# Distances of a graph layer: the right factor by one transpose and masked copies, and one weight load placed a product later

## The chip, the cores and the metric

The kernel runs on one core of one Trainium2 chip. The metric is the device time of one execution in microseconds (us). Before the change three runs gave 1744.81, 1745.28 and 1748.23 us, median 1745.28 us.

A core has five engines that work side by side, each with its own queue of instructions in order: TensorE (PE; its weight loads are shown as PEld), VectorE (DVE), ScalarE (ACT), GpSimd (POOL) and SyncE (SP, which here only issues DMAs). [...]

## The reference, cut to what matters

The layer takes x (32 graphs, 512 nodes, 256 features) and a 0/1 adjacency matrix per graph. After a layer norm and a ReLU (h), three things are made of h and fed to a GRU-like gate block:

```
s     = h @ w_se.T + b_se                       # 3 numbers per node
sq    = sum(s*s, -1)
dist  = sq[:, :, None] + sq[:, None, :] - 2 * einsum('bnd,bmd->bnm', s, s)
A     = exp(-dist) * adj                        # 512 x 512 per graph
x_nmp = A @ relu(h @ w_msg.T + b_msg)
x_conv = relu(bn2(conv17(relu(bn1(conv1(h))))) + h)
gi = [x_conv, x_nmp] @ w_ih.T + b_ih ;  gh = h @ w_hh.T + b_hh
r, z = sigmoid(gi_r + gh_r), sigmoid(gi_z + gh_z)
out = x + (1-z) * tanh(gi_n + r*gh_n) + z*h
```

All arithmetic is float32. The change concerns how -dist is formed for one graph, and where one load of w_hh stands.

## The kernel before, in words

**Stages.** The 32 graphs are worked in two groups of 16. For each group `first_part` makes h, its transpose hT (tile `hT`, PE transposes `phT`), the first convolution (`conv1`, L434) and a transform along the nodes (`windows_to_freq`, L449). Then `nodes` runs over the group's graphs: messages (`message`, L551), distances, the aggregation with A (`aggregate7`, a product of seven block products with sums on POOL, L655), and, spread between, the 40 `product`s of the transformed convolution (L498), which need weights `wt` loaded from DRAM by SP (L460). Group 0 leaves four products over; they run inside group 1's `first_part`. A last stage computes the gates for 16 pairs of graphs.

**Order.** In these stages the order of instructions on every engine is the order of the program text (a manual schedule). The tool puts in the waits. So an instruction that waits holds all that stand behind it on its engine.

**The distances of one graph.** The 512 nodes are held as 4 chunks of 128; node features lie with nodes on partitions. `message` computes for each chunk the 256 message features and the 3 numbers s in one product (L551), and DVE adds the biases into `st` (L553) and into the message tile (L554); ACT applies ReLU to two chunks at a time (L555). `features` squares s on DVE (L562) and lets ACT lay out two tiles: `fl` (L563), 32 columns per chunk of which 9 are used (s, s squared, and a constant -0.5), and `fr` (L565, two copies), the same kind of rows for the right side, written four times over, once for each place the left chunk can have: 4 x 128 columns. `factors` turns `fl` by one PE transpose (L570), evicted by ACT to `sl` (L572), and `fr` by **four** PE transposes (L575), one per chunk, evicted by one ACT copy to `sr`, 128x512 (L577). Row group 32*mc of `sl` then holds the 9 rows of left chunk mc, and the same rows of `sr` hold the right side of all 512 nodes. `exponents` runs four matmuls `pd` over 9 rows each (L593); they start at partitions 0, 32, 64 and 96. ACT takes the exponential (L599), DVE multiplies with the transposed adjacency (L582, L603).

**Around the start of `nodes`** the text order is: all of message of the first graph; its `features`; half of the message of the second graph; `factors` of the first; `by_chunks` of the third (two ACT copies, L536); the other half of the second's message; `features` of the second; `exponents` of the first; and then the loop, which starts with `factors` of the second. In the loop `factors` of a graph stands before one or two products and a message, and its `exponents` behind them.

**Around the load.** In group 1's `first_part` a list `left` holds the four products left over, cut into five fills. With b0 the group's first graph, the text order is:

```
fill 1: load_unit(u2), prepare(u1)
load_x(b0+2)  [SP];  transpose_h(b0);  statistics(b0+1)
fill 2: combine.pop(0), product(u0), prepare(u2)
normalise(b0+1);  statistics(b0+2)
fill 3: product(u1), load_unit(u3)
load_x(b0+3)  [POOL's DMA queue];  conv1(b0)
fill 4: prepare(u3), product(u2)
normalise(b0+2);  transpose_h(b0+1)
fill 5: product(u3)
statistics(b0+3);  transpose_h(b0+2);  normalise(b0+3);  conv1(b0+1);  windows_to_freq(b0)
```

`prepare` does two sums on POOL (L465 `wsum`, needs `wt`; L478 `both`), which the last third of `product` needs. `statistics` ends with a power on POOL (L393). The first entry of `combine` issues one thing: the load of w_hh in four DMAs of 192 KB on POOL's queue (L211), for weight sums that POOL makes later.

Of the kernel before, what the change touches and what calls it, by code (L numbers as in the profile page):

```python
# [11 lines left out]
FP = mybir.dt.float32  # L12
AF = mybir.ActivationFunctionType
ALU = mybir.AluOpType

P = 128
# [146 lines left out]
def gnn_layer(  # L163
# [15 lines left out]
    nc = tc.nc  # L179
    B, N, D = x.shape  # L180
    KT = w2T.shape[1]
    PAD = KT // 2
    NS = w_seT.shape[1]
    DC = D // P
    NC = N // P
# [7 lines left out]
    consts = ctx.enter_context(tc.tile_pool(name="consts", bufs=1))  # L193
    dram = ctx.enter_context(tc.tile_pool(name="dram", bufs=1, space=bass.MemoryType.DRAM))
    psum = ctx.enter_context(tc.tile_pool(name="psum", bufs=8, space=bass.MemoryType.PSUM))
    pools = {}
    outer = ExitStack()
    work = pools["work"] = outer.enter_context(tc.tile_pool(name="work", bufs=2, reuse_waits="tile"))
    early = outer.enter_context(tc.tile_pool(name="early", bufs=1, reuse_waits="tile"))
    wts = outer.enter_context(tc.tile_pool(name="wts", bufs=3, reuse_waits="tile"))  # L200

    def bank(name):
        return psum.tile([P, N], FP, tag="bank", name=name)

    X, ADJ, XN, HT, HQ, H1, MSG, A, NMP, ST, SL, SR = ({} for _ in range(12))
# [12 lines left out]
    ident = consts.tile([P, P], FP, name="ident")  # L218
# [14 lines left out]
    at, cols, n = {}, {}, 0  # L233
# [15 lines left out]

    def vectors():  # L250

        for h in range(2):
            rows = slice(64 * h, 64 * (h + 1))
            nc.gpsimd.tensor_copy(vech[rows].rearrange("p (m e) -> p e m", e=DC),
                                  vec2[rows].rearrange("p e (m h) -> p e m h", h=2)[..., h])
        for name in VEC:
            at[name] = vech[:, cols[name]]
        nc.gpsimd.tensor_add(brz, at["b_ih"][:, : 2 * DC], at["b_hh"][:, : 2 * DC])
        batch_norm("bn2", scale2, shift2, nc.gpsimd)

    def batch_norm(k, scale, shift, engine):
        engine.tensor_scalar(scale, at[k + "_v"], BN_EPS, None, op0=ALU.add)
        nc.gpsimd.tensor_tensor(scale, scale, minus_half[:, :DC], op=ALU.pow)
        engine.tensor_mul(scale, scale, at[k + "_g"])
        engine.tensor_mul(shift, at[k + "_m"], scale)
        engine.tensor_sub(shift, at[k + "_b"], shift)
# [9 lines left out]
    row1 = [bank(f"row1_{i}") for i in range(2)]  # L276
    shift1_row = early.tile([P, D], FP, name="shift1_row")
    def bn1_row(i, v, ones, diags):
        for c in range(DC):
            diag = diags[:, i, c, :]  # L280
            nc.scalar.activation(diag, ident, AF.Copy, scale=v[:, c : c + 1])
            nc.tensor.matmul(row1[i][:, c * P : (c + 1) * P], ones, diag, start=True, stop=True)
# [17 lines left out]
    bmsg = early.tile([P, D + NS], FP, name="bmsg")  # L300
# [16 lines left out]

    fl = early.tile([P, NC, 32], FP, name="fl")  # L320
    fr = early.tile([P, NC, 4, 32], FP, name="fr")
    nc.vector.memset(fl, 0.0)
    nc.vector.memset(fr, 0.0)
    nc.vector.memset(fl[:, :, 2 * NS : 3 * NS], -0.5)
    nc.vector.memset(fr[:, :, :, NS : 2 * NS], -0.5)


    WD = dram.tile([ROWS, D * D + 4 * D], FP, name="wd")
# [197 lines left out]
    def by_chunk(t):  # L526

        return t.rearrange("p (g c k) -> p c g k", g=4, c=NC)

    def chunks(t):  # L530
        return t.rearrange("p (c g k) -> p c g k", g=4, c=NC)

    def by_chunks(b):
# [2 lines left out]
            nc.scalar.copy(chunks(HQ[b][:, ic, :]), by_chunk(HT[b][:, ic, :]))  # L536
        del HT[b]

    def message(b, halves=range(2)):
        if 0 in halves:  # L540
            ST[b] = pools["nodes"].tile([P, 2, NC, NS], FP, tag="st", name=f"st_{b}", bufs=2)
            MSG[b] = pools["nodes"].tile([P, NC, D], FP, tag="msg", name=f"msg_{b}", bufs=3)
        hq = HQ[b]
        h = NC // 2
        for c0 in (h * k for k in halves):
            m = MSG[b][:, c0 : c0 + h, :]
            for j in range(h):
                c = c0 + j
                p = bank(f"pm_{b}_{c}")
                for ic in range(DC):  # L550
                    nc.tensor.matmul(p[:, : D + NS], hq[:, ic, c * P : (c + 1) * P], wmsg[:, ic, :],  # L551
                                     start=(ic == 0), stop=(ic == DC - 1))
                nc.vector.tensor_add(ST[b][:, 0, c, :], p[:, D : D + NS], bmsg[:, D:])  # L553
                nc.vector.tensor_add(m[:, j, :], p[:, :D], bmsg[:, :D])  # L554
            nc.scalar.activation(m, m, AF.Relu)  # L555
        if 1 in halves:
            del HQ[b]

    def features(b):

        st = ST.pop(b)
        nc.vector.tensor_mul(st[:, 1], st[:, 0], st[:, 0])  # L562
        nc.scalar.copy(fl[:, :, : 2 * NS].rearrange("p c (k n) -> p k c n", n=NS), st)  # L563
        for k, at in enumerate((0, 2 * NS)):
            nc.scalar.copy(fr[:, :, :, at : at + NS], st[:, k, :, None, :].to_broadcast([P, NC, 4, NS]))  # L565

    def factors(b):

        p = bank(f"psl_{b}")
        nc.tensor.transpose(p[:, :P], fl.rearrange("p c k -> p (c k)"), ident)  # L570
        t = SL[b] = pools["nodes"].tile([P, P], FP, tag="sl", name=f"sl_{b}", bufs=2)
        nc.scalar.copy(t, p[:, :P])  # L572
        p = bank(f"psr_{b}")
        for c in range(NC):
            nc.tensor.transpose(p[:, c * P : (c + 1) * P], fr[:, c].rearrange("p g k -> p (g k)"), ident)  # L575
        t = SR[b] = pools["nodes"].tile([P, N], FP, tag="sr", name=f"sr_{b}", bufs=2)
        nc.scalar.copy(by_chunk(t), chunks(p))  # L577

    def turn(b, mcs):
        for mc in mcs:  # L580
# [5 lines left out]
    def exponents(b):  # L586

        A[b] = pools["nodes"].tile([P, NC, N], FP, tag="A", name=f"A_{b}", bufs=2)
        sl, sr = SL.pop(b), SR.pop(b)
        pd = [bank(f"pd_{b}_{mc}") for mc in range(NC)]  # L590
        for mc in range(NC):
            rows = slice(32 * mc, 32 * mc + 3 * NS)
            nc.tensor.matmul(pd[mc], sl[rows, :], sr[rows, :], start=True, stop=True)  # L593
        for mc in range(NC):
            if b in in_banks:
                EXP[b, mc] = pd[mc]
            else:
                EXP[b, mc] = A[b][:, mc, :]
            nc.scalar.activation(EXP[b, mc], pd[mc], AF.Exp)  # L599
# [552 lines left out]
    def first_part(g, freq, between, left=()):  # L1152
# [6 lines left out]
        if g == 0:  # L1159
            t = XN[b0] = pools["first"].tile([P, NC, D], FP, tag="xn", name="rows", bufs=2)  # L1160
            ones, diags = t[:, 0, :P], t[:, 1:3, :].rearrange("p i (c m) -> p i c m", m=P)
            nc.vector.memset(ones, 1.0)

            for _ in range(5):
                nc.tensor.matmul(row1[1][:, : 2 * P], ident, fr.rearrange("p c g k -> p (c g k)")[:, : 2 * P], start=True, stop=True)
            batch_norm("bn1", scale1, shift1, nc.gpsimd)
            bn1_row(0, scale1, ones, diags)
            bn1_row(1, shift1, ones, diags)
# [24 lines left out]
        for b in range(b0, b1):  # L1193
            if b + 3 < b1:
                load_x(b + 3, nc.sync if b < 3 else nc.gpsimd)
            if b == b0:
# [13 lines left out]
                xf, last_two = freq(g), two  # L1210
# [62 lines left out]
    with tc.tile_pool(name="freq", bufs=1) as fpool:  # L1273
# [3 lines left out]
        with phase("first", "gen"):  # L1277
# [23 lines left out]
            with tc.manual_schedule():  # L1301
                xf = first_part(0, freq_tile, between)
# [4 lines left out]
        def nodes(g, xf, units, last, following=()):  # L1307
# [45 lines left out]
            for i, b in enumerate(todo):  # L1353
# [24 lines left out]
                if more:  # L1378
                    factors(more[0])
# [32 lines left out]
        with phase("pw", "ahead"):  # L1412
            with phase("seven", "nodes"):
                with tc.manual_schedule():
                    nodes(0, xf, range(UNITS - LEFT), GB, range(UNITS - LEFT, UNITS - LEFT + 2))
            with phase("first", "sums"):
                combine = combine_weights()

                def between(b):

                    if b == GB - 3:
                        for u in range(3):
                            load_unit(1, u)
                    two = [partial(sum_unit, pools["pw"], 1, b - GB + 3)] if b > GB - 3 else []
                    return combine[b - 2] if 1 < b <= len(combine) + 1 else [], two


                pw, (u0, u1, u2, u3) = pools["pw"], range(UNITS - LEFT, UNITS)
                left = [[partial(load_unit, 0, u2, pools["sums"]), partial(prepare, pw, 0, u1, xf)],
                        [*combine.pop(0), partial(product, pw, 0, u0, xf), partial(prepare, pw, 0, u2, xf)],  # L1430
                        [partial(product, pw, 0, u1, xf), partial(load_unit, 0, u3)],
                        [partial(prepare, pw, 0, u3, xf), partial(product, pw, 0, u2, xf)],
                        [partial(product, pw, 0, u3, xf)]]
                prepare(pw, 0, u0, xf)
                with tc.manual_schedule():
                    xf = first_part(1, freq_tile, between, left)
            with phase("seven", "nodes"):
                with tc.manual_schedule():
                    nodes(1, xf, range(UNITS), GB - 3)
# [92 lines left out]
```

## Time and profile before

| | us |
|---|---|
| median of three runs | 1745.28 |
| the profiled execution | 1746.26 |
| its span, first to last instruction | 1744.5 |
| PE busy | 1727.1 |
| DVE busy | 1311.0 |
| POOL busy | 1083.0 |
| ACT busy | 672.6 |

In time order of that span: group 0's `first_part` up to about 157 us, its `nodes` to about 430, group 1's `first_part` to about 549, its `nodes` to about 831, then the gates. The profile page lists busy times, a chain of waits that leads back from the last instruction, and groups of instructions by line; a timeline lists instructions in order with, in brackets, the idle time before them and what ended it. A matmul's busy time includes its way through the array; what a matmul costs on a full PE is the distance from its start to the next one's start.

### The profile page before, as it was taken

The numbers are of one execution on the slowest core, as the hardware profiler recorded it, in microseconds if no ns is written. First come the engines' busy times: TensorE is split into PE (matmuls) and PEld (weight loads), VectorE is DVE, ScalarE is ACT, GpSimd is POOL, SyncE is SP. The second block draws the span as 40 slices with busy tenths as digits, with TensorE's granted clock in tenths as the row PEclk, the third lists the DMA queues.
The fourth block names the chain that finished last, engine by engine and source line by source line (L and its number), as shares of the span: only waits on it lengthen the run. The fifth ranks groups of instructions, "written<-read, shape, count | busy, mean of one in ns | idle before, by whom it ended". The sixth has DMA issues, their size and how long they took to land.

```text
span 1744.5 us, 24392 instructions
## 1 busy us (share of the span) xinstructions
PE 1727.1 (99%) x8006; PEld 1332.3 (76%) x8006; DVE 1311.0 (75%) x2598; ACT 672.6 (39%) x1543; POOL 1083.0 (62%) x1071
## 2 busy tenths in 40 slices
PE   9999999999999999999999999999999999999998
PEld 6677888888898888886877787778777787778754
DVE  7885787777896667766477788777877788777867
ACT  4556545543445544544323231323223232323221
POOL 3431787777655677767866566755676566755551
PEclk9999999999999999999999999999999999999999
DMA  9998988995777988889512442234422442244323
GB/s 250 300 304 237 258 217 249 234 240 175 247 272 203 272 235 235 250 221 291 187 61 67 127 127 74 81 100 127 116 64 75 127 127 71 66 118 127 103 61 73
DMA packets 311682, 295.09 MB, mean 169 GB/s; under 512 B 147436, under 2 KB 241164, under 8 KB 311172
## 3 DMA queue, kind: packets, MB, share of 16 engines
q1 hardware_dynamic: 301588, 265.17, 53.7%
q0 software_dynamic: 6960, 26.65, 4.7%
q10 hardware_dynamic: 3008, 1.72, 0.3%
q8 instruction: 64, 1.05, 0.3%
q14 instruction: 62, 0.51, 0.1%
HBM read 194.31 MB, written 99.16 MB: 168 GB/s over the span
## 4 chain that ended last, share of the span: by engine, by line
PE 91%; DMA 2%; POOL 2%; DVE 2%; SPq 1%; issue 1%; ACT 1%; POOLq 0%; ACTq 0%; DVEq 0%
PE pg L900 29%; PE pn L917 17%; PE py L498 11%; PE pn L655 10%; PE pm L551 6%; PE pc L434 5%; PE pc L863 3%; PE px L449 3%; PE pd L593 2%; PE pw L358 1%; DMA wt<-wd 1%; PE phT L414 1%; PE pg L917 1%; PE pz L917 1%; PE pc L866 1%; PE psr L575 1%
## 5 line engine op out<-in xcount | busy, mean ns | idle before, releaser
L465 POOL TENSOR_TENSOR wsum<-wt 128x512 f32<-128x512 f32 x66 | 91.4, 1385 | 116.9 <-DMA wt<-wd 92.1
L498 PE MATMUL py<-wt,xf 128*128 128x256 f32 x640 | 155.9, 387 | 3.3 <-DMA wt<-wd 3.3
L900 PE MATMUL pg<-te,sw 128*128 128x256 f32 x600 | 154.0, 379 | 0.0
L498 PEld LDWEIGHTS py<-wt,xf 128*128 128x128 f32 x640 | 118.2, 192 | 38.8 <-issue 19.7
L891 ACT ACTIVATE rz<-rz,brz 128x256 f32<-128x256 f32 x180 | 86.4, 504 | 147.9 <-DVE rz L906 147.8
L900 PEld LDWEIGHTS pg<-te,sw 128*128 128x128 f32 x600 | 114.0, 190 | 15.5
L900 PE MATMUL pg<-hn,sw 128*128 128x256 f32 x480 | 123.2, 379 | 0.0
L900 PE MATMUL pg<-tn,sw 128*128 128x256 f32 x480 | 123.2, 379 | 0.0
L603 DVE TENSOR_TENSOR A<-A,at 128x512 f32<-128x512 f32 x124 | 118.7, 995 | 4.2 <-ACT A L599 4.0
L917 PE MATMUL pn<-tn,sw_n 128*128 128x512 f32 x256 | 120.3, 592 | 0.0
L434 PE MATMUL pc<-w,hT 128*128 128x256 f32 x512 | 117.5, 382 | 0.9 <-DVE hT L418 0.9
L551 PE MATMUL pm<-wmsg,hq 128*128 128x259 f32 x512 | 117.5, 381 | 0.0
L1062 ACT ACTIVATE pn<-nt,vech 128x512 f32<-128x512 f32 x45 | 31.1, 692 | 218.2 <-DVE nt L1059 138.9
L434 PEld LDWEIGHTS pc<-w,hT 128*128 128x128 f32 x512 | 94.8, 190 | 23.6 <-issue 7.2
L797 POOL TENSOR_TENSOR tn<-hn 128x512 f32<-128x512 f32 x64 | 87.2, 1381 | 35.7 <-PE pn L917 35.6
L551 PEld LDWEIGHTS pm<-wmsg,hq 128*128 128x128 f32 x512 | 96.5, 190 | 14.7
L900 PEld LDWEIGHTS pg<-hn,sw 128*128 128x128 f32 x480 | 91.2, 190 | 18.3 <-PE pn L917 3.3
L900 PEld LDWEIGHTS pg<-tn,sw 128*128 128x128 f32 x480 | 91.2, 190 | 12.4
L906 DVE TENSOR_TENSOR ct<-pg,ct 128x256 f32<-128x256 f32 x180 | 74.6, 414 | 32.1 <-PE pg L900 22.2
L917 PEld LDWEIGHTS pn<-tn,sw_n 128*128 128x128 f32 x256 | 48.7, 190 | 61.2 <-issue 50.9
L393 POOL TENSOR_TENSOR rstd<-rstd,minus_half 128x4 f32<-128x4 f32 x32 | 33.4, 1042 | 99.0 <-DVE rstd L392 94.2
L917 PE MATMUL pn<-hn,sw_n 128*128 128x512 f32 x192 | 90.3, 592 | 0.0
(229 smaller groups left out, 4386.4 us busy)
## 6 DMA issues: line engine op xcount, KB each, us to landing
wt<-wd SPq DMA_DIRECT2D x80, 512.0 KB, 7.7
adj<-in_adj_dram SPq DMA_DIRECT2D x128, 256.0 KB, 6.5
wd<-wst SPq DMA_DIRECT2D x64, 320.0 KB, 6.4
yd<-y SPq DMA_DIRECT2D x76, 256.0 KB, 5.9
hd<-hT SPq DMA_DIRECT2D x32, 512.0 KB, 4.4
nd<-nmp SPq DMA_DIRECT2D x32, 512.0 KB, 3.0
xb<-in_x_dram SPq DMA_DIRECT2D x128, 128.0 KB, 4.8
out_dram<-xb SPq DMA_DIRECT2D x122, 128.0 KB, 2.3
```

Source lines behind the costliest of these rows:

```text
L434: nc.tensor.matmul(p[:, j, :], HT[b][:, ic, c * P : (c + 1) * P], w1[:, ic, :], start=(ic == 0), stop=(ic == DC - 1))
L449: nc.tensor.matmul(p[:, j * 2 * L : (j + 1) * 2 * L], H1[b][:, c0 + j, ic * P : (ic + 1) * P], fwd, start=True, stop=True)
L465: nc.gpsimd.tensor_tensor(t, WT[g, u][:, 0], WT[g, u][:, 1], op=ALU.add)
L498: nc.tensor.matmul(dst, v[:, ic, :], w[:, ic, :], start=(ic == 0), stop=(ic == DC - 1))
L551: nc.tensor.matmul(p[:, : D + NS], hq[:, ic, c * P : (c + 1) * P], wmsg[:, ic, :], start=(ic == 0), stop=(ic == DC - 1))
L603: nc.vector.tensor_mul(A[b][:, mc, :], EXP.pop((b, mc)), AT.pop((b, mc)))
L655: nc.tensor.matmul(bk, left[:, k, :], right[:, k, :], start=(first and k == 0), stop=(k == 1), skip_group_check=True)
L797: nc.gpsimd.tensor_tensor(dst[:, k], x[:, k], y[:, k], op=op)
L891: nc.scalar.activation(at(dst), at(src), AF.Sigmoid, bias=brz[:, o : o + 1], scale=sign)
L900: nc.tensor.matmul(bk, SW["hk"][:, k, s, :], c if k == 2 else hn[:, k], start=(onto is None and k == 0), stop=(k == K3 - 1), skip_group_ch ...
L906: nc.vector.tensor_tensor(at(dst), at(x), at(y), op=op)
L917: nc.tensor.matmul(bk[:, t], weight(q, k, o), terms[k][q][:, t], start=(first and i == 0), stop=(i == len(ks) - 1), skip_group_check=True)
```

## The change

The features have eight rows per chunk in place of nine of 32 (s in three, the sum of squares in one, a constant in one, three unused). `fl` and `fr` are laid out as four places of four chunks of eight rows: `fl` repeats the left chunk's eight rows four times in its place, `fr` holds the eight rows of each right chunk, the same in every place. One transpose turns `fr`; four ACT copies with a per-partition scale write `sr`, the one for chunk c keeping only the rows of chunk c (`mask`, a column of ones and zeros, made once) and zeroing the others. The matmuls `pd` then run over 32 rows. The squares move from DVE to ACT (into a tile `SQ`), and DVE sums them. The warm-up matmuls at the kernel's start become ten of 128 columns in place of five of 256. The load of w_hh moves from the head of fill 2 to the end of fill 3.

```diff
     def vectors():
+        nc.vector.tensor_reduce(mask, ident.rearrange("p (g c k) -> p c g k", g=4, c=NC), mybir.AxisListType.XY, ALU.add)
...
-    fl = early.tile([P, NC, 32], FP, name="fl")
-    fr = early.tile([P, NC, 4, 32], FP, name="fr")
+    fl = early.tile([P, 4, NC, 8], FP, name="fl")
+    fr = early.tile([P, 4, NC, 8], FP, name="fr")
     nc.vector.memset(fl, 0.0)
     nc.vector.memset(fr, 0.0)
-    nc.vector.memset(fl[:, :, 2 * NS : 3 * NS], -0.5)
-    nc.vector.memset(fr[:, :, :, NS : 2 * NS], -0.5)
+    nc.vector.memset(fl[:, :, :, NS + 1], -0.5)
+    nc.vector.memset(fr[:, :, :, NS], -0.5)
+    mask = consts.tile([P, NC], FP, name="mask")
...
     def message(b, halves=range(2)):
...
-                nc.vector.tensor_add(ST[b][:, 0, c, :], p[:, D : D + NS], bmsg[:, D:])
+                nc.vector.tensor_add(ST[b][:, c, :NS], p[:, D : D + NS], bmsg[:, D:])
                 nc.vector.tensor_add(m[:, j, :], p[:, :D], bmsg[:, :D])
+            if c0 > 0:
+                SQ[b] = work.tile([P, NC, NS], FP, tag="sq", name=f"sq_{b}")
+                nc.scalar.activation(SQ[b], ST[b][:, :, :NS], AF.Square)
             nc.scalar.activation(m, m, AF.Relu)
...
     def features(b):
         st = ST.pop(b)
-        nc.vector.tensor_mul(st[:, 1], st[:, 0], st[:, 0])
-        nc.scalar.copy(fl[:, :, : 2 * NS].rearrange("p c (k n) -> p k c n", n=NS), st)
-        for k, at in enumerate((0, 2 * NS)):
-            nc.scalar.copy(fr[:, :, :, at : at + NS], st[:, k, :, None, :].to_broadcast([P, NC, 4, NS]))
+        nc.vector.tensor_reduce(st[:, :, NS], SQ.pop(b), mybir.AxisListType.X, ALU.add)
+        nc.scalar.copy(fl[:, :, :, : NS + 1], st[:, :, None, :].to_broadcast([P, NC, NC, NS + 1]))
+        nc.scalar.copy(fr[:, :, :, :NS], st[:, None, :, :NS].to_broadcast([P, 4, NC, NS]))
+        nc.scalar.copy(fr[:, :, :, NS + 1], st[:, None, :, NS].to_broadcast([P, 4, NC]))
...
     def factors(b):
...
         p = bank(f"psr_{b}")
-        for c in range(NC):
-            nc.tensor.transpose(p[:, c * P : (c + 1) * P], fr[:, c].rearrange("p g k -> p (g k)"), ident)
-        t = SR[b] = pools["nodes"].tile([P, N], FP, tag="sr", name=f"sr_{b}", bufs=2)
-        nc.scalar.copy(by_chunk(t), chunks(p))
+        nc.tensor.transpose(p[:, :P], fr.rearrange("p g c k -> p (g c k)"), ident)
+        t = SR[b] = pools["nodes"].tile([P, N], FP, tag="sr", name=f"sr_{b}", bufs=2)
+        for c in range(NC):
+            nc.scalar.activation(by_chunk(t)[:, c], p[:, :P].rearrange("p (g k) -> p g k", g=4), AF.Copy,
+                                 scale=mask[:, c : c + 1])
...
-            rows = slice(32 * mc, 32 * mc + 3 * NS)
+            rows = slice(32 * mc, 32 * mc + 32)
             nc.tensor.matmul(pd[mc], sl[rows, :], sr[rows, :], start=True, stop=True)
...
-            for _ in range(5):
-                nc.tensor.matmul(row1[1][:, : 2 * P], ident, fr.rearrange("p c g k -> p (c g k)")[:, : 2 * P], start=True, stop=True)
+            for _ in range(10):
+                nc.tensor.matmul(row1[1][:, :P], ident, fr.rearrange("p g c k -> p (g c k)"), start=True, stop=True)
...
                 left = [[partial(load_unit, 0, u2, pools["sums"]), partial(prepare, pw, 0, u1, xf)],
-                        [*combine.pop(0), partial(product, pw, 0, u0, xf), partial(prepare, pw, 0, u2, xf)],
-                        [partial(product, pw, 0, u1, xf), partial(load_unit, 0, u3)],
+                        [partial(product, pw, 0, u0, xf), partial(prepare, pw, 0, u2, xf)],
+                        [partial(product, pw, 0, u1, xf), partial(load_unit, 0, u3), *combine.pop(0)],
                         [partial(prepare, pw, 0, u3, xf), partial(product, pw, 0, u2, xf)],
```

More of the change, by code (lines that the diff above doesn't have):

```diff
@@ L537, in by_chunks @@
         del HT[b]
+    SQ = {}
     def message(b, halves=range(2)):
         if 0 in halves:
-            ST[b] = pools["nodes"].tile([P, 2, NC, NS], FP, tag="st", name=f"st_{b}", bufs=2)
+            ST[b] = pools["nodes"].tile([P, NC, NS + 1], FP, tag="st", name=f"st_{b}", bufs=2)
             MSG[b] = pools["nodes"].tile([P, NC, D], FP, tag="msg", name=f"msg_{b}", bufs=3)
@@ L561, in features @@
         st = ST.pop(b)
-        nc.vector.tensor_mul(st[:, 1], st[:, 0], st[:, 0])
-        nc.scalar.copy(fl[:, :, : 2 * NS].rearrange("p c (k n) -> p k c n", n=NS), st)
-        for k, at in enumerate((0, 2 * NS)):
-            nc.scalar.copy(fr[:, :, :, at : at + NS], st[:, k, :, None, :].to_broadcast([P, NC, 4, NS]))
+        nc.vector.tensor_reduce(st[:, :, NS], SQ.pop(b), mybir.AxisListType.X, ALU.add)
+        nc.scalar.copy(fl[:, :, :, : NS + 1], st[:, :, None, :].to_broadcast([P, NC, NC, NS + 1]))
+        nc.scalar.copy(fr[:, :, :, :NS], st[:, None, :, :NS].to_broadcast([P, 4, NC, NS]))
+        nc.scalar.copy(fr[:, :, :, NS + 1], st[:, None, :, NS].to_broadcast([P, 4, NC]))
     def factors(b):
         p = bank(f"psl_{b}")
-        nc.tensor.transpose(p[:, :P], fl.rearrange("p c k -> p (c k)"), ident)
+        nc.tensor.transpose(p[:, :P], fl.rearrange("p g c k -> p (g c k)"), ident)
         t = SL[b] = pools["nodes"].tile([P, P], FP, tag="sl", name=f"sl_{b}", bufs=2)
```

## The prediction, made before the result was known

> **What bounds the kernel now.** First the page's busy times and, from its part 4, the chain of waits.
>
> ```profile
> PE 1727.1 (99%) x8006; PEld 1332.3 (76%) x8006; DVE 1311.0 (75%) x2598; ACT 672.6 (39%) x1543; POOL 1083.0 (62%) x1071
> ...
> PE 91%; DMA 2%; POOL 2%; DVE 2%; SPq 1%; issue 1%; ACT 1%; POOLq 0%; ACTq 0%; DVEq 0%
> ```
>
> PE sets the time nearly everywhere, so an instruction taken from PE counts at its full distance to the next one, unless PE then waits where it did not. Next, what the transposes cost there: PE's timeline in the middle of group 1.
>
> ```profile
> 595.28 0.27 PE L570 MATMUL psl<-ident,fl 128*128 128x128 f32 x1
> 595.39 0.60 PE L575 MATMUL psr<-ident,fr 128*128 128x128 f32 x4
> 595.83 1.03 PE L498 MATMUL py<-wt,xf 128*128 128x256 f32 x4
> ```
>
> Left factor, right factor, next product: four transposes take 595.39 to 595.83, 0.11 us each. (0.27 is one's way through the array, not its price.) Third, PE's longest wait, which lies at the moved load: the timelines of PE and of POOL, and the windows, whose last three columns are granted clock, DMA share and GB/s.
>
> ```profile
> 441.97 1.04 PE L414 MATMUL phT<-ident,xn 128*128 128x128 f32 x8
> 446.29 3.61 PE L498 MATMUL py<-wt,xf 128*128 128x256 f32 x8 [3.28 <-DMA wt<-wd]
> 449.74 1.03 PE L498 MATMUL py<-wsum,both 128*128 128x256 f32 x4
> ```
>
> ```profile
> 436.64 2.19 POOL L211 DMA_DIRECT2D w<-in_w_hhT_dram  x4
> ...
> 440.93 1.03 POOL L393 TENSOR_TENSOR rstd<-rstd,minus_half 128x4 f32<-128x4 f32 x1
> 441.93 0.82 POOL L215 DMA_DIRECT2D x<-in_x_dram  x1
> 446.32 1.26 POOL L465 TENSOR_TENSOR wsum<-wt 128x512 f32<-128x512 f32 x1 [3.58 <-DMA wt<-wd]
> ```
>
> ```profile
> 443.00:446.30 3.30, 0.02 (x2) 0.04 (x1) 2.36 (x7) 0.91 (x3) 0.00 (x0) 0.99 0.95 315
> 446.30:449.70 3.40, 3.40 (x8) 2.74 (x9) 0.88 (x2) 0.00 (x0) 2.66 (x3) 0.51 0.47 184
> ```
>
> PE stands 3.28 us for the weights of the last left-over product (u3; SP issued them at 433, landing took 13.2 us), and then runs 3.4 us at a granted clock of 0.51, so 8 passes take 3.4 us from start to start instead of 1.73: 1.7 us more. Together 5.0 us. The four w_hh DMAs come in between: from 439.5 to 446.2 the DMA view gives POOL's queue 1.28 MB and SP's only 0.14 MB.
>
> **Part A, the distances.**
>
> *Removed from PE*: 3 transposes x 32 graphs x 0.109 us (0.44 / 4) = **10.5 us**.
>
> *The `pd` matmuls* run over 32 rows, not 9, from the same start partitions. Eight passes of 512 columns now take 1.07 us from their start to the next product's (602.02 to 603.09), since four run side by side. I take nothing for the rows. The other end: eight passes one behind the other at 0.43 us (the distance of L638's 512-column passes) are 3.4 us, 2.4 us a graph, 75 us in all. The nearest row is these matmuls themselves, so I give that end 1 in 100 and leave it out of the range.
>
> *Added on ACT.* The form of the masked copies, an activation with a per-partition scale, 128x128, stands once in the trace, at the start.
>
> ```profile
> L281 ACT ACTIVATE rows<-ident,bn_scale x2: 384/392/401, 4.5 to 4.8; 128x128 f32<-128x128 f32 x2
> ...
> L281 ACT ACT_TABLE_LOAD  x1: 1283/1283/1283, 1.7 to 1.7; - x1
> ```
>
> They start 0.29 us apart; four hold the queue 1.16 us, where the one copy held it 0.48 (164.43 to 164.91, below): +0.68 us. The plain 128x128 copy (0.265 us, 0.14 apart) bounds it below at +0.1; 0.40 each, unpipelined, above at +1.1. The square is an ACT instruction on 12 elements: 0.1 us of queue by the small copies L563 and L565. Their own sizes (24, 48, 48 become 64, 48, 16 elements) cancel. So +0.8 us of ACT a graph, about 25 us in all.
>
> In the loop it is hidden: `sr` ends at 596.6 and the next ACT copy starts at 597.8, and `pd` reads `sr` only at 602.0. The square falls into 1.06 us in which ACT waited for DVE before the second ReLU. Without that cover each 0.1 us that reaches PE costs 3.2 us over 32 graphs.
>
> At the start of `nodes` there is no cover. ACT's and PE's timelines there:
>
> ```profile
> 164.43 0.59 ACT L577 COPY sr<-psr 128x512 f32<-128x512 f32 x1
> 164.91 1.15 ACT L536 COPY hq<-hT 128x512 f32<-128x512 f32 x2
> 166.00 0.63 ACT L555 ACTIVATE msg<-msg 128x512 f32<-128x512 f32 x1
> 166.54 0.20 ACT L563 COPY fl<-st 128x24 f32<-128x24 f32 x1
> ```
>
> ```profile
> 166.79 0.33 PE L570 MATMUL psl<-ident,fl 128*128 128x128 f32 x1 [0.27 <-ACT fl L563]
> ```
>
> ACT runs without a pause and PE already waits for it. `fl` comes 0.68 + 0.1 later, the left transpose at 167.58; the third layout copy ends near 167.75, so the next message starts near 167.9 against 167.56 now, +0.35, where two graphs' transposes should have brought -0.65. Loss 1.0 us; group 1 has the same rows at 558: **2.0 us**.
>
> *DVE.* The reduction replaces L562 (0.15 to 1.25 us, mean 0.66 by its group). Its bounds: 0.15 (aggregating 128x6) and the 1.25 it replaces; I take 0.16 in most graphs, no slower. It is a new wait of DVE on ACT, with the next graph's adds or the adjacency transposes queued behind it; the square should be done before DVE has finished the add L554. The mask's reduction, once, lies between that 0.15 and 0.43 (statistics over 256): hidden, DVE is busy 30 of 40 us there. The smaller clears save 0.3 us of DVE before x has landed; the warm-up keeps its number of columns and ends before the first `phT`, which waited 0.46 us for `xn`: nothing, or up to 2 us if its 20 weight loads of 0.34 us go one by one (1.9 + 6.7, against 6.1 for the 10 passes now, less that wait).
>
> *Given back to POOL.* Twice PE waits for a POOL sum (0.47 us at 212, 0.61 at 422), whose chain starts behind earlier PE work with one graph's transposes in between: 0.33 each, **0.7 us**.
>
> A = 10.5 - 2.0 - 0.7 = **7.8 us**; bounds 5 (`nodes` starts worse, 0.1 us shows in half the graphs) and 10.5.
>
> **Part B, the load.** SP's order is untouched; the load is passed on POOL by `wsum` and `both` of u2 and by the power of `statistics(b0+2)`. By 439.5 nearly all of u3's weights had moved; the rest, 0.14 MB, trickled beside w_hh. With w_hh away they land near 441-442, before PE's need at 443.0. But POOL is late next. The power still ends at 441.96 (it waits for x through DVE); w_hh 2.19 -> 444.15; x(b0+3) 0.82 -> 444.97; `wsum` 1.26 and `both` 0.72 -> 446.9. PE runs two thirds of u3 from 443.0 to 444.75, waits 2.2 us, and ends at 446.95 + 0.86 = 447.8, against 450.6 now: 2.8 us. Behind the four issues on POOL's queue is x(b0+3), 2.2 us later; landing in 6.0 us as now, it comes at 450.2. DVE takes it up at 451.30 now and `xn` ends 4.6 us later, at 455.88; PE needs it at 457.1, or 454.3 with the gain: 0.5 us late. B = 2.8 - 0.5 = **2.3 us**. Bounds: 5.0 if all of the wait goes; -1.7 if 2.2 us of waiting still halves the clock and x lands past 452 (no row shows either, waits up to 0.61 us left the clock at 1.00).
>
> [...]
>
> **Sum.** 7.8 + 2.3 = 10.1 us. The profiled execution took 1746.26 us (span 1744.5), so 1736.2; it lies 1.0 us over the median of the runs, 1745.28. Against that median: **1735.2 us**. Range of this case: 1732 to 1739.
>
> **Rivals.**
>
> *Table switches (slower).* If `Square` does not share ACT's table with `Exp`, each graph loads two tables. For it: a load is 1.283 us (L281's row). Against it: between 1.7 and 841 us there is no other, though copy, ReLU, identity and exponential alternate; `Square` is not among these, so no row settles it. Price: 2.57 us more before `p<-pn` (L660), where ACT idles 1.27 us; the copy would end 1.3 us later, at 608.0, and PE's next product into that bank starts at 607.51: 0.5 us x 30 graphs = 16, and 2 x 2.6 at the starts, 21 in all: 1735.2 + 21 = 1756 us. It decides from 0.34 us a graph on.
>
> [...]
>
> *The saved PE time turns into other waits.* DMA is 0.90 busy in these stages and POOL waited 92 us for `wt`; if loads set the pace, A goes to 0-3 and the time is 1740-1743. Against: PE itself waited for `wt` once only, at 443.
>
> *Everything is kept.* ACT has more room than I think and u3 never waits: 10.5 + 5.0 = 15.5, 1729.8.
>
> *The change does not do what it says*: the wait at 443 remains and only A counts: 1737.5, inside the first range.
>
> **Chances.** Forecast 0.63 (with the last rival); other waits 0.16; everything kept 0.13; table switches 0.05; serial `pd` 0.01; others near no change 0.02. Range 1730.5 to 1741, which leaves out the slower cases and half of the two neighbours. 0.2% is 3.5 us, about what can be told from no change. Faster 0.90, same 0.05, slower 0.05.
>
> **What would show it.** `psr` x32 at 0.11 us; masked copies x128 near 0.39 us or less; no table load between 1.7 and 830 us; a longer wait before `psl` at the two starts; at about 439.5 (group 0 being 3.5 us shorter) no wait for `wt` but one of about 2 us for POOL's `both`, and full clock. A wait of PE before `pd` on `sr`, or before L655 on `p`, in every graph would prove me wrong.

## The result, and the profile after

The changed kernel took 1738.3 us in the median of five runs (1737.52 to 1740.9), beside 1744.81 us for the kernel before (five runs, 1742.04 to 1748.23): a ratio of 0.9965, 95% interval 0.9949 to 0.9981. Forecast were 1735.2 us, 10.1 less than before; measured are 6.5 less. The time lies inside the range, and 3.1 us above the forecast.

The profiled execution took 1737.52 us (span 1735.7), against 1746.26 (span 1744.5) before. First the page: busy times and the shares of the chain of waits.

```profile
PE 1718.5 (99%) x7920; PEld 1323.0 (76%) x7920; DVE 1300.2 (75%) x2599; ACT 692.6 (40%) x1671; POOL 1086.8 (63%) x1071
...
PE 93%; DVE 2%; POOL 2%; DMA 1%; ACT 1%; SPq 1%; issue 1%; POOLq 0%; DVEq 0%; ACTq 0%
```

PE has lost 8.6 us of busy time, and the span has lost 8.8. ACT has gained 20 us and 128 instructions, and its share of the chain is what it was. Next the new operations: the groups of the tiles `psr`, `sr` and `sq`, as least/median/most ns of one, then the first and the last start.

```profile
L587 ACT ACTIVATE sr<-psr,mask x128: 368/377/461, 167.7 to 807.9; 128x128 f32<-128x128 f32 x128
...
L584 PE MATMUL psr<-ident,fr x32: 272/272/329, 166.3 to 806.7; 128*128 128x128 f32 x32
```

```profile
L604 PE MATMUL pd<-sr,sl x256: 587/625/692, 168.9 to 810.9; 32*128 32x512 f32 x128
```

```profile
L564 ACT ACTIVATE sq<-st x32: 196/212/244, 164.9 to 799.5; 128x12 f32<-128x12 f32 x32
L572 DVE TENSOR_REDUCE st<-sq x32: 166/167/168, 165.1 to 799.7; 128x4 f32<-128x12 f32 x32
```

The masked copies take 0.377 us each (0.39 forecast), the matmuls over 32 rows what those over 9 rows took (587/625/693 before), the sum on DVE 0.167. There is no table load between 1.67 and 832.83 us. From graph to graph PE's starts fall back by 0.33 us against before, which is three transposes at 0.11. The rows of the graph that the prediction showed at 595 us:

```profile
590.33 0.27 PE L584 MATMUL psr<-ident,fr 128*128 128x128 f32 x1
590.44 1.89 PE L503 MATMUL py<-wt,xf 128*128 128x256 f32 x8
```

The next product starts 0.11 us behind the right factor's transpose, where it was 0.44.

The start of `nodes`, timelines of ACT and of PE:

```profile
167.69 1.14 ACT L587 ACTIVATE sr<-psr,mask 128x128 f32<-128x128 f32 x4
168.70 1.16 ACT L541 COPY hq<-hT 128x512 f32<-128x512 f32 x2
```

```profile
168.89 1.46 PE L604 MATMUL pd<-sr,sl 32*128 32x512 f32 x8 [0.51 <-ACT sr L587]
170.68 0.33 PE L580 MATMUL psl<-ident,fl 128*128 128x128 f32 x1 [0.33 <-ACT fl L573]
```

Four copies hold ACT's queue 1.01 us, from 167.69 to 168.70 (1.16 forecast). PE now waits twice, 0.51 us for `sr` and 0.33 for `fl`, where one wait of 0.27 stood. The same pair comes at group 1's start, 0.52 and 0.34; there PE's own row names DVE for the first, and the row of its weight load names `sr`.

The load, in POOL's timeline and then PE's:

```profile
439.41 2.19 POOL L211 DMA_DIRECT2D w<-in_w_hhT_dram  x4
441.59 0.80 POOL L215 DMA_DIRECT2D x<-in_x_dram  x1
442.41 1.27 POOL L470 TENSOR_TENSOR wsum<-wt 128x512 f32<-128x512 f32 x1
443.63 0.79 POOL L483 TENSOR_TENSOR both<-xf 128x256 f32<-128x256 f32 x1
```

```profile
440.62 1.89 PE L503 MATMUL py<-wt,xf 128*128 128x256 f32 x8
444.47 1.13 PE L503 MATMUL py<-wsum,both 128*128 128x256 f32 x4 [1.97 <-POOL both L483]
```

As forecast, the weights are there, POOL is late, PE waits about 2 us and keeps its full clock behind it.

What no step of the forecast named lies far from both edits, at 74 us, in group 0's `first_part`. Windows of the changed kernel (length, then busy time and number of instructions of PE, PEld, DVE, ACT, POOL; granted clock, DMA share, GB/s):

```profile
71.00:74.40 3.40, 3.08 (x16) 1.49 (x15) 1.21 (x3) 3.40 (x10) 2.34 (x5) 1.00 1.06 145
74.40:77.80 3.40, 3.40 (x16) 1.56 (x14) 3.37 (x13) 0.91 (x2) 0.90 (x1) 0.50 0.98 343
77.80:81.20 3.40, 3.40 (x12) 2.69 (x9) 2.20 (x6) 1.55 (x3) 0.94 (x2) 0.50 1.06 354
```

The same for the kernel before:

```profile
71.00:74.40 3.40, 3.08 (x16) 1.50 (x15) 1.21 (x3) 3.40 (x10) 2.35 (x5) 1.00 1.06 141
74.40:77.80 3.40, 3.40 (x23) 2.28 (x22) 3.37 (x13) 2.38 (x5) 0.90 (x1) 1.00 0.98 324
```

The first stretch looks the same in both. Behind it the changed kernel runs at half clock for 6.83 us, starts 16 matmuls where before starts 23, and is 3.27 us later from there on. The median missed the forecast by 3.1 us.

### The profile page after: what moved, and what is told of

Its sections match the earlier page's. It is cut to its first block, busy times and chain, and to the rows that moved or that the text cites. A ratio compares the mean times of both kernels' runs of the same rounds, so it can differ in the third digit from the quotient of the medians.

```text
span 1735.7 us, 24321 instructions
## 1 busy us (share of the span) xinstructions
PE 1718.5 (99%) x7920; PEld 1323.0 (76%) x7920; DVE 1300.2 (75%) x2599; ACT 692.6 (40%) x1671; POOL 1086.8 (63%) x1071
## 4 chain that ended last, share of the span: by engine, by line
PE 93%; DVE 2%; POOL 2%; DMA 1%; ACT 1%; SPq 1%; issue 1%; POOLq 0%; DVEq 0%; ACTq 0%
PE pg L911 29%; PE pn L928 17%; PE py L503 11%; PE pn L666 10%; PE pm L558 6%; PE pc L439 5%; PE px L454 3%; PE pc L874 3%; PE pd L604 2%; PE pw L363 2%; PE phT L419 1%; PE pg L928 1%; PE pz L928 1%; PE pc L877 1%; POOL tn L808 0%
```

## The experiments

Three questions: what each edit is worth alone, where the 2 us at u3 go, and what brings the half clock. The first four kernels ran beside 23 runs of the kernel before, median 1743.29 us; the next four beside 27, median 1741.56; the last three beside 11, median 1741.73. A run's mean granted clock hints at a half clock: 6.83 us at half in 1736 are 0.002. Of the profiled runs those at 0.998 and 0.999 had none (but the 3.4 us at u3 in before), those at 0.995 to 0.997 had one of 6.83 us or more. (The last 3 to 6 us of every profile, where PE runs out of work, are at half clock and left out here.)

**1. The distances alone** (w_hh at its old place).

```diff
-                        [partial(product, pw, 0, u0, xf), partial(prepare, pw, 0, u2, xf)],
-                        [partial(product, pw, 0, u1, xf), partial(load_unit, 0, u3), *combine.pop(0)],
+                        [*combine.pop(0), partial(product, pw, 0, u0, xf), partial(prepare, pw, 0, u2, xf)],
+                        [partial(product, pw, 0, u1, xf), partial(load_unit, 0, u3)],
```

> Only the distances are changed; the w_hh load stays at the head of fill 2. My account of the profile after: distances -9.9 us (10.5 of transposes, less about 0.9 of waits at each of the two starts of nodes, plus a POOL wait of about 0.8 that went), load -2.9, and +3.3 from 6.8 us at half clock in group 0's first_part (74.4 to 81.2), where the kernel before ran at full clock. Theory (the half clock there is a matter of where the clock's own window falls, not of the edit): 1734.9 us when the clock stays full at 74, 1738.2 when not; the wait of 3.28 us before the last left-over product and the half clock behind it are back. Rival 1 (the distances edit itself brings the half clock, always): every run near 1738.2. Rival 2 (the transposes were hidden and all the gain was the load): 1744.8.

Measured: 1734.59 us (six runs, 1732.98 to 1739.97), ratio 0.9954, interval 0.9938 to 0.9969. So this edit brings 8.7 us against the median beside it, a little more than the 7.8 forecast, and all of what the whole change brings. The profiled execution (1733.24) has no half clock at 74. At u3, with the load still at its old place, PE's wait is not the 3.28 us of before:

```profile
437.48 1.97 PE L503 MATMUL py<-wt,xf 128*128 128x256 f32 x8 [1.18 <-DVE y L512]
```

```profile
437.51 1.28 POOL L470 TENSOR_TENSOR wsum<-wt 128x512 f32<-128x512 f32 x1 [2.11 <-DMA wt<-wd]
```

It is 1.18 us, with no half clock behind it. PE's row names DVE, which was done at 437.35; POOL's `wsum` reads the same weights, starts at the same moment (437.51) and names them, so I take the wait to be for `wt`.

**2. The load alone** (all of the distances as before).

```diff
-                        [*combine.pop(0), partial(product, pw, 0, u0, xf), partial(prepare, pw, 0, u2, xf)],
-                        [partial(product, pw, 0, u1, xf), partial(load_unit, 0, u3)],
+                        [partial(product, pw, 0, u0, xf), partial(prepare, pw, 0, u2, xf)],
+                        [partial(product, pw, 0, u1, xf), partial(load_unit, 0, u3), *combine.pop(0)],
```

> Only the w_hh load is moved; the distances are as before. Theory: PE waits about 2.0 us for POOL's sum both instead of 3.28 us for weights, and no half clock follows: -2.9 us, 1741.9 us in runs with full clock at 74. Rival 1 (half clock at 74 belongs to the distances): no run of this kernel shows it, all near 1741.9. If it is a matter of the window, some runs show it and lie 3.3 us higher, near 1745. Rival 2 (the later load of x takes the gain back): 1744.8.

Measured: 1744.23 us (12 runs, 1741.17 to 1745.83), ratio 1.0001, interval 0.9991 to 1.001. The moved load by itself brings nothing that can be told. My sum for it fell. Its profile has the wait for POOL, as theory says:

```profile
448.30 1.13 PE L498 MATMUL py<-wsum,both 128*128 128x256 f32 x4 [1.44 <-POOL both L478]
```

It also has the half clock, from 74.56 for 6.83 us, with the old distances. So the new distances aren't needed for it.

**3. The load one step later still**, behind `prepare(u3)`.

```diff
-                        [partial(product, pw, 0, u1, xf), partial(load_unit, 0, u3), *combine.pop(0)],
-                        [partial(prepare, pw, 0, u3, xf), partial(product, pw, 0, u2, xf)],
+                        [partial(product, pw, 0, u1, xf), partial(load_unit, 0, u3)],
+                        [partial(prepare, pw, 0, u3, xf), *combine.pop(0), partial(product, pw, 0, u2, xf)],
```

> The changed kernel with the w_hh load one step later still, behind prepare(u3) on POOL's queue, so that POOL makes wsum and both of u3 before it issues the four DMAs. Theory (the 1.97 us wait before the last third of u3 is POOL's queue, 2.19 us of DMA issues ahead of the sums): the wait goes, 2.0 us less than the changed kernel, 1736.3 us; x(b0+3) is no longer behind w_hh. Rival (the wait is the landing of u3's weights, which POOL's sum needs): no change, 1738.3, and the wait stays near 2 us.

Measured: 1734.47 us (five runs, 1732.48 to 1737.19), ratio 0.9948, interval 0.9934 to 0.9962. In PE's timeline u3 runs without a break:

```profile
440.55 1.89 PE L503 MATMUL py<-wt,xf 128*128 128x256 f32 x8
442.28 1.03 PE L503 MATMUL py<-wsum,both 128*128 128x256 f32 x4
```

What is late next is 0.21 us before a transpose at 457, which waits for `xn`. So the wait in the changed kernel is the four DMA issues on POOL's queue in front of `wsum`, as argued. The time by itself doesn't show it: four of the five runs have a clock of 0.999, and their median, 1734.11, is about that of the two runs of the changed kernel at 0.999 in experiment 5, which were not taken beside them. Experiments 9 and 10 were, and show it. The profiled run was the one of five at 0.997, and had the half clock (75.26 to 82.09).

**4. The masked copies twice**, to find what their price is.

```diff
-        for c in range(NC):
+        for c in (*range(NC), *range(NC)):
             nc.scalar.activation(by_chunk(t)[:, c], p[:, :P].rearrange("p (g k) -> p g k", g=4), AF.Copy,
```

> The changed kernel with the four masked copies of the right factor made twice: +1.16 us of ACT for each of 32 graphs. Theory (hidden in the loop, seen only at the two starts of nodes, where ACT runs without a pause): about +1.2 us at each start, +2.4 us, 1740.7 us. Rival (the copies reach PE in every graph): up to 32 x 1.16 = 37 us, 1775 us.

Measured: 1739.2 us (12 runs, 1734.48 to 1742.2), ratio 0.9975, interval 0.9966 to 0.9985. The start of `nodes`, on PE:

```profile
165.53 1.46 PE L604 MATMUL pd<-sr,sl 32*128 32x512 f32 x8 [1.54 <-ACT sr L587]
```

1.0 us more of ACT turns the wait of 0.51 into 1.54, here and at group 1's start (1.55). Of the other 30 graphs one shows a wait for `sr` (0.59 us at 399). So the cover in the loop holds for twice the work, and the price lies at the two starts. By the ratios the time is some 1.7 us over the changed kernel's, with 2.4 forecast. Nine of its 12 runs have a clock of 0.995 to 0.997; the profiled one, 0.999, isn't among them, so where they lost it stays open.

**5. The changed kernel again.**

> The changed kernel once more, beside the others. Theory (the half clock at 74.4 depends on the phase of a free-running window): not every run has it; runs with a mean granted clock of 0.999 take about 1734, those at 0.996 or 0.997 about 1738, and the median lies between, by how many there are of each. Rival (the changed kernel always brings it): all runs at 0.996 or 0.997 and a median of 1738.

Measured: 1736.62 us (five runs, 1733.43 to 1737.58), ratio 0.9967, interval 0.9954 to 0.9979. Two runs have a clock of 0.999 and took 1733.43 and 1734.7; three have 0.996 or 0.997 and took 1736.62 to 1737.58. The half clock is not in every run, and costs about 3 us.

**6. The right factor transposed four times** (three results aren't read).

```diff
-        nc.tensor.transpose(p[:, :P], fr.rearrange("p g c k -> p (g c k)"), ident)
+        for c in range(NC):
+            nc.tensor.transpose(p[:, c * P : (c + 1) * P], fr.rearrange("p g c k -> p (g c k)"), ident)
```

> The changed kernel with the right factor transposed four times into four places of the bank, of which only the first is used; all else as changed. Theory (part A is worth what three transposes less take on TensorE, 96 x 0.109 us): 10.5 us over the changed kernel, so 1744 to 1748, near the kernel before or over it, since the masked copies' price stays. Rival (those transposes lay in TensorE's waits and the gain came from elsewhere, such as the smaller products or fewer DVE elements): 0 to 3 us over the changed kernel.

Measured: 1743.95 us (11 runs, 1742.38 to 1746.19), ratio 1.0014, interval 1.0006 to 1.0023. That is 7.3 us over the changed kernel's median beside it, and 9.9 over its two runs at 0.999 (10 of these 11 have 0.998 or more). Theory said 10.5; the difference lies in the starts, where the three transposes fill part of the wait for `sr` (0.19 and 0.21 us instead of 0.51 and 0.52). The gain is the transposes'.

**7. Work put into the window at 72 us.** In the step of the product `pw` that starts at 72.14, one matmul of ident by ident ahead of each of the four real ones.

```diff
             p = bank(f"pw_{pc}_{i}_{q}")
+            if (pc, i) == (3, 0):
+                nc.tensor.matmul(p[:, :P], ident, ident, start=True, stop=True)
             nc.tensor.matmul(p[:ROWS, :], taps[32 * q : 32 * q + KT, :],
```

> The changed kernel with four matmuls more, 128 columns each, put in front of the four real ones of the product pw at 72 us of group 0 (their result is overwritten). Theory (the half clock at 74.4 in the profile of the changed kernel comes from how much TensorE does in the stretch from 71 to 74.4, which the phase of a repeating 3.41 us window cuts out): the added passes fill it, no run has the half clock there, every run's mean granted clock is 0.999, and the time is that of the changed kernel less 3.3 us plus at most 0.9 (4 x 0.22): 1734 to 1735.5. Rival (the half clock has nothing to do with those passes): half clock in as many runs as the changed kernel beside it, and a time 0 to 0.9 us above it.

Measured: 1744.04 us (11 runs, 1739.69 to 1745.06), ratio 1.0009, interval 1.0 to 1.0017. Neither theory nor rival: 7.4 us over the changed kernel, and a clock of 0.994 to 0.997 in every run. PE's timeline says why:

```profile
74.96 0.49 PE L364 MATMUL pw<-ident 128*128 128x128 f32 x2
75.38 1.08 PE L365 MATMUL pw<-w2p,taps 17*80 17x512 f32 x2
```

The `pw` matmuls use 17 rows each, in four row groups, and eight passes run in 2.05 us (72.14 to 74.19 in the changed kernel; of the eight at 75.94 the first four start within 0.02 us). With a full matmul between them they no longer overlap: a pair takes 1.01 us, and the added one 0.42, which I had put at 0.22 or less. So the step grew to 7.05 us (73.53 to 80.58, part of it at half clock), filled mostly with passes over 17 rows. The windows:

```profile
74.23:77.64 3.41, 3.41 (x10) 1.02 (x8) 0.69 (x1) 2.00 (x6) 0.71 (x3) 1.00 1.01 214
77.64:81.05 3.41, 3.41 (x7) 1.31 (x7) 0.36 (x1) 0.58 (x1) 0.00 (x0) 0.50 0.93 368
```

PE is busy for all of 74.23 to 77.64, at full clock, and then gets half the clock for 10.24 us. So busy time alone isn't what the clock follows. The number below does better: rows times columns that the passes started in a window feed, times the columns they stream, as a share of full 128x128 passes at 512 columns in 0.43 us (a `pw` pass counts 17 x 80 / 16384 = 0.083). It is taken on a grid of 3.413 us that starts where the trace first grants the full clock; every later change of the clock lies on that grid (in before 129, 130 and 508 steps from its start, in the changed kernel 20, 22 and 505). The table has the first window under 0.40 in 70 to 78 us:

| kernel (profiled execution) | work in the window | half clock behind it |
|---|---|---|
| before | 0.32 | no |
| before, again (11) | none under 0.40 | no |
| distances alone | none under 0.40 | no |
| copies twice | 0.36 | no |
| changed / again | 0.30 / 0.31 | 6.83 us, both |
| load alone / load later | 0.30 / 0.34 | 6.83 us, both |
| four transposes | 0.31 | 6.83 us |
| work put in (7) / with load later (8) | 0.18 / 0.23 | 10.24 us, both |
| work added elsewhere (9) / with load later (10) | none under 0.40, both | no |

The count sorts the windows, but has no sharp edge: 0.32 and 0.36 kept the clock, 0.34 lost it. Taken over all windows at full clock of the 13 profiles, all 16 under 0.30 had half clock behind them and none of some 6500 over 0.36 had. In between both occur: two at 0.31, near the ends of 7 and 9, kept the clock, and one at 0.35, at the start of 7, lost it for 3.41 us. In the first window at half clock the count was low as well (0.27 to 0.30 in the five dips of 6.83 us, 0.15 and 0.24 in 7 and 8), and the window after it was at half clock too. In the changed kernel that second window counts 0.50, and the full clock was back behind it.

Between the profiles of before and of the changed kernel the stretch is the same, and the grid differs: it starts at 5.90 us in before and at 6.13 in the changed kernel, and cuts the stretch 0.23 us later. Elsewhere the stretch itself differs. The grids of the distances alone (5.86) and of the four transposes (5.85) are alike, but the first has no wait of PE between 67 and 75 us and counts 0.45, and the second has one of 0.32 us and counts 0.31.

**8. The later load with the same added work**, meant as the version to beat both.

> The run with the w_hh load behind prepare(u3), which had no POOL wait at u3, and the four extra matmuls at 72 us together. Theory: no half clock and no wait of 2 us, 1732.5 to 1734, below both kernels. Rival (one or both of the two do nothing that lasts): the time of the changed kernel beside it, 1734 to 1738.

Measured: 1743.12 us (11 runs, 1740.99 to 1745.63), ratio 1.0007, interval 0.9998 to 1.0016: as slow as 7, for the same reason (a pair takes 1.01 us here too, and the added matmul 0.41 or 0.42).

**9. Work added where it breaks no overlap**: three matmuls behind the last `px` of the sixth graph, into columns that nothing reads, where PE waits 0.32 us.

```diff
                                      fwd, start=True, stop=True)
+                if (b, ic, c0) == (5, DC - 1, NC - per):
+                    for _ in range(3):
+                        nc.tensor.matmul(p[:, per * 2 * L : per * 2 * L + P], ident, ident, start=True, stop=True)
                 w = w0 + 2 * c0
```

> The changed kernel with three matmuls more of 128 rows and 128 columns, put behind the last px matmul of the sixth graph (at 71.8 us), into columns of its bank that nothing reads; TensorE waits 0.32 us there, so they cost at most 0.3 us. A window's work is counted here as rows times columns that the passes feed, as a share of full passes (512 columns in 0.43 us). In all nine profiles so far a window of 3.41 us with under about 0.32 of full work between 70 and 82 us was followed by one at half clock, whatever TensorE's busy time, and those with 0.32, 0.36 or over 0.40 (before, double copies, distances alone) were not. Theory: six passes of 128 full rows add 0.19 to 0.30, no run has the half clock at 74, the mean granted clock is 0.998 to 0.999 in all runs, and the time is that of the changed kernel's undisturbed runs, 1733.5 to 1735. Rival (any insertion here brings or keeps the half clock, as the four interleaved ones did): 1737 to 1741.

Measured: 1735.09 us (five runs, 1734.91 to 1736.12), ratio 0.9957, interval 0.9944 to 0.997. Four of five runs at 0.999, one at 0.997. In the profiled one the window on the grid stays at full clock, and so does what follows it:

```profile
71.51:74.92 3.41, 3.41 (x23) 1.91 (x26) 1.85 (x4) 3.14 (x8) 1.54 (x4) 1.00 0.97 154
```

This doesn't show that the added work did it. In this execution the added passes start at 70.98, so five of the six fall into the window ahead, and this one counts 0.41 with a single one of them. Four of five stand against two of ten for the changed kernel, but experiments 1 and 3, with nothing added, kept the clock in 9 of 11. "No run" was wrong too. Its wait at u3 was 2.65 us, with no half clock behind it.

**10. The later load and that work.**

> The w_hh load behind prepare(u3), and the three extra matmuls at 71.8 us. Theory: neither a wait of 2 us at u3 nor a half clock at 74: 1732 to 1734, below both kernels, and all runs with a mean granted clock of 0.998 to 0.999. Rival (the fill does nothing): as the later load alone, 1732.5 to 1737 with the half clock in some runs.

Measured: 1734.02 us (six runs, 1732.2 to 1738.66), ratio 0.9952, interval 0.9939 to 0.9964; one run at 0.997. Lower than the changed kernel's ratio (0.9965 and 0.9967), but the intervals overlap, and the later load alone (0.9948) does as much. Against experiment 9 beside it, whose load stands one step earlier, the runs at 0.998 and more are 1.8 us lower (1733.29 against 1735.07 in the median): about the wait for POOL that is gone from its profile.

**11. The kernel before once more.**

> The kernel before once more, for the wait at u3 (443 us). Theory (the weights' landing varies from run to run, so that the prediction's 3.28 us was one draw): a wait other than 3.28 us by over 0.5, without a half clock behind it if it is under 2 us. Rival (the wait belongs to the kernel): 3.1 to 3.4 us and half clock behind it.

Measured: 1741.27 us. PE at u3:

```profile
442.45 1.89 PE L498 MATMUL py<-wt,xf 128*128 128x256 f32 x8
444.36 1.13 PE L498 MATMUL py<-wsum,both 128*128 128x256 f32 x4
```

No wait at all, and no half clock. The weights took 8.5 us from issue to landing here, and 13.2 us in the other execution. The wait that my load's gain was worked out from is there in one execution and not in the next.

## Why the prediction was right, and where it was not

**The transposes (10.5 us): right.** 0.33 us a graph in the traces, and 9.9 us when three are put back (6).

**`pd` over 32 rows, the masked copies in the loop, the sum on DVE: right.** No row moved, and the cover on ACT holds for twice the copies (4). The table switches did not come: ACT loads a table at 1.67 us and next at 832.83, with the 32 squares (164.9 to 799.5) and the exponentials between them.

**The starts of `nodes` (2.0 us): about right.** I gave +0.35 to the next message's start; it is +0.28. But half of it comes as a wait for `sr` (0.51), which I had not named: I followed `fl` alone.

**Given back to POOL (0.7 us): wrong in size.** The wait at 422 grew by 0.17 (0.61 to 0.78). The one at 212 went, but it wasn't there in the second execution of before either. A, forecast 7.8, measures 8.7 between medians, and 9.4 between the runs at 0.998 and more (1733.25 against 1742.7).

**Part B (2.3 us): the mechanism right, the sum wrong.** Between the two profiles it came as forecast: 3.0 us at u3 (PE's lead over before goes from 2.23 to 5.26 us), and even the 0.5 us for the late x is not there, since PE goes into its transposes at 451.94 without a wait. Over the runs it did not. The step that failed is "PE stands 3.28 us ... together 5.0 us", which took one execution's wait for a constant of the kernel. With the load at its old place PE lost 3.28 us (and 1.7 at half clock), 1.18 and 0 in three profiles; at its new place 1.97, 1.80, 1.44, 1.41, 1.34, 2.03 and 2.65 in seven, none with half clock behind it. That a wait of 2.2 us would leave the clock full, as the sum takes it, no run had shown when it was made: 0.61 us had, and 3.28 had not. The old order leaves the wait to how the weights happen to land; the new one takes a sure wait for POOL, about as long as the other is on average in these few profiles (1.8 us, against 2.1 with the clock's share). The load alone measures 1.0001, so B is 0 with about 1.6 us either way. The lower bound of -1.7 had room for it; the value didn't.

**The half clock at 74 us: not foreseen, 3.3 us.** With it the sum comes near: 9.4 for the distances, 0 for the load, less 3.3 (all five runs of the result have a clock of 0.996 or 0.997) gives 6.1, against the 6.5 measured. The sum isn't sharper than about 2 us: at full clock the changed kernel's two runs in experiment 5 are 7.5 us under before beside them (1734.07 against 1741.53), not 9.4, and the medians of before in the four sets of runs go from 1741.56 to 1744.81. The row was to be had: the timeline of before at 70 to 74.4 holds two waits of PE (0.41 and 0.32 us) and passes over 17 rows. That the window's phase and the small waits decide is argued from the table, not shown by a run that sets either. Whether the change makes it more frequent stays open: clocks under 0.998 came in 8 of 10 runs of the changed kernel, in 2 of 11 of experiments 1 and 3, which are in the same order until 430 us, in 1 of 11 of experiment 6 and 9 of 12 of experiment 4, in the same order until 157, in 4 of 12 of the load alone and in 11 of the 61 of before beside the experiments. Where in those runs the clock fell, at 74 us, at u3 or elsewhere, only a profile of each would show.

**The rivals.** "Other waits take it back" has a part in it: not DMA at large, but one wait moved from a DMA to POOL. "Everything is kept" fell with that wait, and serial `pd` and table switches fell. Nearest to the measured time lies the sum of the last rival, 1737.5, in which only A counts, though its condition didn't come: the wait for weights was gone from the profile, and one for POOL stood in its place.

**Luck.** That the time lies in the range is in part luck: A came out larger than forecast by 0.9 to 1.6 us, while B, which was to bring 2.3, brought nothing that can be told, and the half clock took 3.3.

## What to carry to other kernels

Where a wait ends with a DMA in a stage whose DMA engines are 0.9 busy, one execution shows one draw (3.28 us here, and 0 in the next one of the same kernel): look at a second one before the wait is priced, and compare with the sure wait that a new order brings. The work moved from the bounding engine to an idle one cost where a pipeline starts (PE waited 0.51 and 0.33 us there, and not in the loop), so price it there, for each of the tiles that the first user waits for. Busy TensorE is not worked TensorE: in 7 it was busy for all 3.41 us of a window with 0.18 of full work in it, and had half the clock behind it. Look for stretches of few-row passes with small waits in them before you add or take work around them, and mind that a full matmul put between matmuls that share the array by row groups ended their overlap here (1.01 us for each two passes, where eight had taken 2.05).

## What the runs showed of the hardware that was not expected

- TensorE's granted clock went from 1.00 to 0.50 behind a window in which it was busy 3.41 of 3.41 us, with passes over 17 rows by 80 columns in most of it (7). The lengths at half clock were 3.41, 6.83 and 10.24 us, one to three times 3.413.
- The windows at 70 to 75 us sort better by the count of experiment 7 with the transposes `phT` counted in full: without them the windows of the copies twice and of the distances alone have 0.20 and kept the clock, and that of the four transposes has 0.28 and lost it.
- One 128x128 matmul put between matmuls of different row groups cost, beside its own passes, their overlap: from 2.05 us for eight passes to 1.01 us for each two, and 0.42 for the matmul itself (7).
- The same 512 KB of weights, issued at the same place of the program, made PE wait 3.28, 1.18 and 0 us in three executions with the w_hh load at its old place. In the two of the kernel before they were issued at 432.98 and 432.51 us and took 13.2 and 8.5 us to land.
